# Five sums for four in layer 2, three joins for two in layer 1: moving 14 gathers of a graph network from GpSimd to TensorE

## The chip, the cores and the metric

The kernel runs on one NeuronCore of a Trainium2 chip. The metric is device time in microseconds (us) of one execution; lower is better. A core has five engines that run side by side, each with its own instruction stream: TensorE (PE in the profile; its weight loads are PEld), VectorE (DVE), ScalarE (ACT), GpSimd (POOL) and SyncE (SP). SP, ACT and GpSimd also issue DMA transfers, each in the order of its own stream. An instruction that waits for a semaphore holds up everything behind it in its stream.

## What is computed

Two layers of a relational graph convolution over 12,500 nodes with 128 features, 200,000 edges sorted by their target node `dst`, and 8 relations; then a residual sum and a layer norm.

```
def _rgcn_conv(x, src, dst, et, basis, comp, root, bias):
    W = jnp.einsum('rb,bio->rio', comp, basis)
    xw = jnp.einsum('ni,rio->nro', x, W)
    msgs = xw[src, et]
    seg = dst * N_REL + et
    summed = jax.ops.segment_sum(msgs, seg, num_segments=N_NODES * N_REL)
    cnt = jax.ops.segment_sum(jnp.ones((msgs.shape[0],), x.dtype), seg, num_segments=N_NODES * N_REL)
    mean = summed / jnp.maximum(cnt, 1.0)[:, None]
    agg = mean.reshape(N_NODES, N_REL, HIDDEN).sum(axis=1)
    return agg + x @ root + bias
...
h = x
for l in range(2):
    h_new = _rgcn_conv(h, src, dst, edge_type, basis[l], comp[l], root[l], bias[l])
    h = jax.nn.relu(h_new) + h
return _layernorm(x + h)
```

## The kernel before

**Tiles and quads.** The edges lie in 1563 tiles of 128, in their given order. Eight tiles make a quad, so there are 196 quads (0 to 195) in each layer, and each layer's main loop takes one quad a turn. For every edge a row of 128 floats is needed: in layer 1 the row of its source node in `x`, in layer 2 the row of source and relation in a table `y_d` that layer 1 writes to DRAM (each node's `h` times each relation's weight).

**The usual way to the rows: a gather.** `gather` (line 786) has GpSimd issue an indirect DMA for each tile, 128 rows picked by a column of indices, on line 814. A quad's rows go into one of seven buffers (`rows_r`, `AHEAD` + 2). `gathers` (line 837) writes the gathers of quad q + 5 into the program at turn q, so that of the seventh quad on waits until TensorE has used the buffer. For the last six quads (`NQ - LATE`, that is from quad 190 on) it is quad q + 2 that is written at turn q, and line 825 adds a wait for whatever quad TensorE was last told to use by then (the cell `("done", l)`).

**What TensorE does with them.** VectorE makes a weighted one-hot matrix of each tile's target nodes (`onehot`, line 1240: four quads' worth of buffers in layer 1, two in layer 2). In layer 1 `means` (line 1340) multiplies rows and one-hots, ACT copies the result, `product` (line 1372) multiplies with the relations' weights, ACT copies again and `place` (line 1403) adds to the node tile's sum; `table` (line 1558) makes the rows of `y_d`. In layer 2 `add_rows` (line 1726) multiplies rows and one-hots straight into the node tile's sum; `finish` adds the carry and the residual, and `norm` does the layer norm of eight node tiles at a time, whose result SP stores and whose buffer SP then loads with later rows of `x`.

**Three other ways to the rows**, each of which spares GpSimd its gathers:

- *Single-row lists* (`lists`, line 692; `lone_rows`, line 727). Every so many tiles a tile's 128 rows are fetched by 128 DMAs of one row each, issued by SP or by ACT (line 750) after a load of 32 addresses at a time (line 745). In layer 2 SP has tiles 62, 111, 160 and so on (every 49th, 31 tiles) and ACT has 63, 112 and so on. A chunk of 32 rows stands in the program up to 15 quads ahead of the quad that needs it; four tiles of a list have a place of their own (the halves of the buffers `sT`). `add_rows` waits for all the rows of its quad, these too.
- *Joins* in layer 1 (`JOINED`, `joining`, line 1475). For four tiles at once: the edges' sources are compared with the node numbers of each of the 98 node tiles (VectorE, line 1516), and each comparison is multiplied with that tile of `x` (TensorE, line 1531), which sums up the wanted rows. An entry holds the first tile served, and the first and last quad over which the 98 steps are spread. Two entries: eight tiles.
- *Sums* in layer 2 (`SUMMED`, `summed`, line 1586). The same for a whole quad, from `h` in SBUF: per node tile a transpose of `h` (TensorE, line 1610), its copy (VectorE, line 1618), a comparison of 1024 edges (line 1619), and two matmuls of 512 columns (line 1628); at the end the result is turned, multiplied with weighted one-hots and with the relations' weights. `52: (3, 45)` means that quad 52 is served by steps over quads 3 to 45. Four entries: 32 tiles.

**The order** on each engine is written out by the two loops at the end of `ordered_path`: what a turn calls first stands first in every engine's stream. `Plan.add` derives the waits from the cells that an operation reads and writes.

Of the kernel before, what the change touches and what calls it, by code (L numbers as in the profile page):

```python
# [428 lines left out]
def ordered_path(  # L429
# [26 lines left out]
    P = 128  # L456
# [11 lines left out]
    Q = 8  # L468
# [20 lines left out]
    SOON = 16  # L489
    DONE = NT - 4  # L490
    LONG = 9
    JOINED = [(1112, 84, 132), (1504, 135, 183)]
    SUMMED = {52: (3, 45), 98: (49, 91), 144: (95, 137), 190: (141, 183)}
    assert D == P and R * K == P and B == BF + 1 and 1 < TL and LAST < P and BF % 4 == 0 and Q == G and N % 2 == 0
    main = slice(HALO, HALO + P)

# [77 lines left out]
    def part_of(n, *cell):  # L574
        nonlocal free_at
        free_at += n
        assert free_at <= at
        used_c.append(cell)
        return arena[:, free_at - n:free_at], cell

    M = 4
    xb_b = [part_of(S * D, "xb", i) for i in range(2)]
    eqb_b = [part_of(M * P, "eqb", i) for i in range(4)]
    ends_b = part_of(M * P, "ends")
    joined_b = [part_of(M * P, "joined", i) for i in range(len(JOINED))]
    joined = {t + i: (joined_b[k][0][:, i * P:(i + 1) * P], [joined_b[k][1]])
              for k, (t, _, _) in enumerate(JOINED) for i in range(M)}
    room_c += used_c
    p_8 = keep([P, S + 2], F32, "p_8")
# [2 lines left out]
    first = keep([P, B], F32, "first")  # L592
# [86 lines left out]
    def floats(t, n):  # L679
        return t[:, n * P:(n + 1) * P]  # L680

    sT_f = [t.rearrange("p r g k -> p (r g k)") for t in sT_r.tiles]
# [6 lines left out]
    def hot_cells(c):  # L689
# [4 lines left out]
                                     (sel.rearrange("p g k -> p (g k)"), ["sel"], [])]),  # L694
         ("ACT", 13 * Q + 2, 46 * Q, 8 * Q, 16, 10, [(floats(yr_f, j), yr_cells, yr_cells) for j in range(5)]),
         ("ACT", 53 * Q + 2, 1552, 8 * Q, 16, 10, [(floats(mixer_f, j), ["mixer"], []) for j in range(2)])],
        [("SP", 62, 1552, 49, 32, 15, [(floats(sT_f[0], j), [("sT", 0, 0), ("sT", 0, 1)], []) for j in range(4)]),
         ("ACT", 63, 1552, 49, 32, 15, [(floats(sT_f[1], j), [("sT", 1, 0), ("sT", 1, 1)], []) for j in range(4)])]]
    single, at_row = [{}, {}], [0, 0]
    for l in range(L):  # L700
        for k, (_, t0, t1, by, _, _, hosts) in enumerate(lists[l]):
# [84 lines left out]
    def gather(l, q):  # L786
        if q >= NQ or l == 1 and q in SUMMED:
            return
# [433 lines left out]
    dms, sT, ys, pl, ym = {}, {}, {}, {}, {}  # L1222
    acc, carry, vs, xs, xT, wide = {}, {}, {}, {}, {}, {}

    def onehot(l, q, g=None):

        if q >= NQ and (g is None or g < 0) or l == 1 and q in SUMMED:
            return
# [246 lines left out]
    def joining(k):  # L1475

        tile0, first, end = JOINED[k]
        n = end - first + 1
        slots = [(g, i) for g in range(NX) for i in range(shape_of(g)[1])]
        assert len(slots) == NT  # L1480
        takes = {q: [] for q in range(first - 1, end + 3)}
        for j in range(NT):
            takes[first + j * n // NT].append(j)
        used = {g: [q for q, js in takes.items() if any(slots[j][0] == g for j in js)] for g in range(NX)}
        loads = {}
        for g in range(NX):
            loads.setdefault(max(first - 4 + g, JOINED[k - 1][2] + 2 if k else 0) if g < 2 else used[g - 2][-1] + 2, []).append(g)
        (e_t, e_c), (f_t, f_c), (j_t, j_c) = ends_b, eqb_b[0], joined_b[k]
        f3, j3 = (t.rearrange("p (t c) -> p t c", t=M) for t in (f_t, j_t))
        b, bc = ct_b  # L1490
        done = end + 1
        assert max(len(v) for v in takes.values()) <= 2
        assert tile0 // Q >= done + 3 and (k == 0 or first >= JOINED[k - 1][2] + 3)

        def load_b(g):
            p, m = shape_of(g)
            t, c = xb_b[g % 2]
            load(t[:p, :m * D], in_rows(x, g), [], [c] + (free_c if k == 0 and g < 2 else []), "ACT")

        def start_of(q):  # L1500
            if q == first - 4:
                assert checked and parts is None
                load(j_t.bitcast(I32), bass.AP(tensor=src.tensor, offset=src.offset + tile0 * P,
                                               ap=[[0, P], [1, M * P]]), [], [j_c] + free_c, "ACT")
            for g in loads.get(q, ()):
                load_b(g)

        def before(q):
            if q == first - 2 and k == 0:
                x_nodes()  # L1510
            if q == first:
                vec(lambda: nc.vector.tensor_copy(e_t, j_t.bitcast(I32)), [j_c], [e_c] + (free_c if k == 0 else []))
            for j in takes.get(q, ()):
                p = shape_of(slots[j][0])[0]
                o, oc = eqb_b[j % 4]
                vec(lambda j=j, p=p, o=o: nc.vector.tensor_tensor(  # L1516
                    o[:p], e_t[:p], x_node[:p, j:j + 1].to_broadcast([p, M * P]), op=ALU.is_equal),
                    [e_c, "x_node"], [oc])
            if q == done + 1:
                vec(lambda: nc.vector.tensor_copy(f3, b), [bc], [f_c])  # L1520
            if q == done + 2:
                vec(lambda: nc.vector.tensor_copy(j3, b), [bc], [j_c])
            plan.mark("DVE")

        def after(q):
            for j in takes.get(q - 1, ()):
                g, i = slots[j]
                p, m = shape_of(g)
                t, c = xb_b[g % 2]
                o, oc = eqb_b[j % 4]  # L1530
                pe(lambda j=j, p=p, i=i, t=t, o=o: nc.tensor.matmul(  # L1531
                    b.rearrange("p t c -> p (t c)"), t[:p, i * D:(i + 1) * D], o[:p], start=j == 0, stop=j == NT - 1),
                    [c, oc], [bc])
            if q == done + 1:
                pe(in_turn([lambda i=i: nc.tensor.transpose(b[:, i, :], f3[:, i, :], ident) for i in range(M)]),
                   [f_c, "ident"], [bc])
            plan.mark("PE")

        return start_of, before, after

    joins = [joining(k) for k in range(len(JOINED))]

    def join(o, part):
        for (_, first, end), f in zip(JOINED, joins):
            if first - 4 <= o <= end + 3:
                f[part](o)
# [135 lines left out]

    sums_of = [(s - 1, *summed(i, s, *SUMMED[s])) for i, s in enumerate(sorted(SUMMED))]

    def summing(q, part):
        for end, *f in sums_of:
            if SUMMED[end + 1][0] - LONG <= q <= end:
                f[part](q)
# [18 lines left out]
    def add_rows(q, k, opens, last, between_last=None):  # L1707
        if q in SUMMED:
            place_sums(q, k, opens, last)
# [159 lines left out]
    def run(gen, n):  # L1869
        for _ in range(n):  # L1870
            if next(gen, gen) is gen:
                return True
        return False
# [49 lines left out]
    later = checks()  # L1923
# [32 lines left out]
    for o in range(NG - 3):  # L1956
        if o + CLOSE == NQ - 2:
            gather(0, NQ - 1)
        gathers(0, o)
        means(o)  # L1960
        batch(o)
        join(o, 0)
        if o == 1:
            where()
            load_offsets()
        if o > 1:
            lone_rows(0, "SP", o)
        for i in range(2 if o < FIRST else 1):
            if parts is not None and run(parts, 1):
                parts = None  # L1970
        onehot(0, o + 2, o - 1)
        join(o, 1)
        if parts is None:
            run(later, 3 if o < 84 else 1)
        if o > 1:
            lone_rows(0, "ACT", o)
        if not opened:
            end()
        for step in opened:
            step()  # L1980
        opened.clear()
        if o > 0:
            product(o - 1)
            if o < SOLO:
                take_product(o - 1)
            else:
                late_y.append(o - 1)
        for step in behind:
            pe(*step)
            plan.mark("PE")  # L1990
        behind.clear()
        join(o, 2)
        if o > 1:
            k = place(o - 2)
            close(k)
            if k is not None and k % S == S // 2 and k // S + 1 < NX:
                n = k // S + 1
                turned_to.extend([turn_x(n, h) for h in range(-(-shape_of(n)[1] // 4))])
                turned_to.append((lambda n=n: load_x(n + 1), None))
        for i in range(2):  # L2000
            if turned_to:
                a, b = turned_to.pop(0)
            elif tables and o >= TABLE and (i == 0 or len(tables) > 6 or o > NG - 16):
                a, b = tables.pop(0)
            else:
                break
            while copies:
                copies.pop(0)(vcopy)
            a()
            if b is not None:  # L2010
                copies.append(b)
# [69 lines left out]
    for q in range(NQ):  # L2081
# [4 lines left out]
        k = sup(q)  # L2086
# [116 lines left out]
```

## Time and profile before

| what | value |
|---|---|
| three runs | 3728.68, 3730.01, 3738.03 us; median 3730.01 |
| the profiled execution's own time | 3738.43 us |
| its span, first to last instruction | 3736.6 us |
| busy share of PE, DVE, ACT, POOL | 80%, 63%, 9%, 75% |
| layer 1's gathers / layer 2's gathers | 1499 / 1469 |
| mean granted clock of TensorE | 0.937 |

How to read it: a group's row gives the line of the kernel, the engine, what is written from what, the count, then busy time and mean duration in ns, then the idle time of that engine just ahead of these instructions and what ended it. "issue" there means that the engine waited for nothing that the profile shows. A row of a line's or tile's view gives the count, the least, median and largest duration in ns, and when the first and the last began. A timeline's row gives the start, the length and what ran, neighbours of one kind merged; names with a q (SPq, ACTq) are an engine's sequencer issuing DMAs.

### The profile page before, as it was taken

How to read it: one execution, taken by the hardware profiler on the slowest of the kernel's cores; microseconds unless marked ns; L12 is line 12 of the kernel's file. 1: busy time of each engine (PE TensorE's matmuls, PEld its weight loads, DVE VectorE, ACT ScalarE, POOL GpSimd, SP SyncE). 2: the span in 40 equal slices, each digit the busy share in tenths (PEclk: the TensorE clock that was granted, in tenths of full speed). 3: DMA queues.
4: the chain of work that ended last, by engine and by line, in shares of the span. 5: the costliest groups of instructions: out<-in, count | busy, mean ns of one | idle time of the engine just before them, and what ended most of it. 6: DMA issues, size and time to landing. Idle time of an engine off the chain costs nothing.

```text
span 3736.6 us, 69352 instructions
## 1 busy us (share of the span) xinstructions
PE 2986.0 (80%) x13831; PEld 2137.2 (57%) x13831; DVE 2354.0 (63%) x5786; ACT 354.5 (9%) x795; POOL 2812.0 (75%) x2977
## 2 busy tenths in 40 slices
PE   5777757778877778877778888888888888798896
PEld 3666645565655556655555555555555555555554
DVE  5556435545554445445456778787777787787885
ACT  1121212111111111111100000000000000000000
POOL 7777777777777777777777777777777777777776
PEclk7999889989999999999989999999999999999998
DMA  4122123334333333332332222222222222222222
GB/s 126 55 62 61 56 89 106 117 115 123 112 101 100 91 104 106 95 106 92 99 97 56 55 56 67 67 62 67 56 73 62 62 67 62 67 66 56 68 66 61
DMA packets 159970, 299.91 MB, mean 80 GB/s; under 512 B 67108, under 2 KB 90358, under 8 KB 159534
## 3 DMA queue, kind: packets, MB, share of 16 engines
q0 software_dynamic: 95008, 194.77, 20.4%
q10 hardware_dynamic: 34755, 68.94, 5.7%
q1 hardware_dynamic: 29771, 31.73, 3.2%
q14 instruction: 325, 2.66, 0.2%
q8 instruction: 111, 1.82, 0.2%
HBM read 236.52 MB, written 58.65 MB: 79 GB/s over the span
## 4 chain that ended last, share of the span: by engine, by line
POOL 47%; issue 17%; PE 16%; DMA 9%; ACTq 4%; ACT 3%; DVE 2%; SPq 1%; POOLq 0%; DVEq 0%
POOL rows L814 47%; DMA rows<-y_d,idy 7%; PE y L1372 4%; ACTq L750 3%; PE s L1340 3%; PE s L1726 2%; PE pt L1558 1%; ACTq L745 1%; PE ct L1531 1%; ACT sT L663 1%; SPq L750 1%; ACT y_row L663 1%; DVE dm L1240 1%; PE ct L1010 1%; PE ct L1011 1%
## 5 line engine op out<-in xcount | busy, mean ns | idle before, releaser
L814 POOL DMA_INDIRECT rows<-in_x_dram,idx x1499 | 1420.0, 947 | 459.8 <-issue 451.1
L814 POOL DMA_INDIRECT rows<-y_d,idy x1469 | 1390.0, 946 | 449.8 <-issue 440.2
L1726 PE MATMUL s<-dm,rows 128*128 128x256 f32 x2932 | 777.2, 417 | 260.7 <-DMA rows<-y_d,idy 235.8
L1240 DVE TENSOR_SCALAR dm<-cols,near,w 128x256 f32<-128x256 f16 x1531 | 709.6, 537 | 386.1 <-PE s L1726 376.4
L1726 PEld LDWEIGHTS s<-dm,rows 128*128 128x128 f32 x2932 | 592.4, 210 | 376.4 <-DMA rows<-y_d,idy 233.7
L1240 DVE TENSOR_SCALAR dm<-cols,kr,w 128x128 f32<-128x128 f16 x1563 | 525.9, 403 | 137.4 <-PE s L1340 112.5
L1372 PE MATMUL y<-w_sb,sT 128*128 128x128 f32 x3136 | 443.8, 300 | 203.9 <-ACT ys L663 150.6
L1372 PEld LDWEIGHTS y<-w_sb,sT 128*128 128x128 f32 x3136 | 406.7, 209 | 240.3 <-ACT ys L663 177.6
L1340 PEld LDWEIGHTS s<-dm,rows 128*128 128x128 f32 x2998 | 382.2, 201 | 184.0 <-issue 159.1
L1340 PE MATMUL s<-dm,rows 128*128 128x128 f32 x2998 | 401.6, 287 | 100.5 <-DMA rows<-in_x_dram,idx 90.4
L1619 DVE TENSOR_TENSOR arena<-arena,cols 128x1024 f32<-128x1024 int32 x264 | 319.9, 1212 | 0.0
L1628 PE MATMUL pt<-arena,idx 128*128 128x512 f32 x528 | 269.6, 592 | 0.0
L1628 PE MATMUL y<-arena,idx 128*128 128x512 f32 x528 | 269.6, 592 | 0.0
L1558 PE MATMUL pt<-w_sb,arena 128*128 128x512 f32 (+1 forms) x386 | 206.3, 616 | 63.0 <-DVE y_row L666 43.9
L666 DVE COPY y_row<-pt 128x512 f32<-128x512 f32 x56 | 38.7, 692 | 309.9 <-PE pt L1558 309.9
L663 ACT ACTIVATE sT<-s 128x512 f32<-128x512 f32 x391 | 213.4, 605 | 87.0 <-PE s L1340 86.7
L1516 DVE TENSOR_TENSOR arena<-arena,cols 128x512 f32<-128x512 f32 (+1 forms) x196 | 125.7, 683 | 115.0 <-PE ct L1531 112.2
L1531 PE MATMUL ct<-arena 128*128 128x512 f32 x392 | 187.1, 600 | 0.0
L663 ACT ACTIVATE y_row<-pt 128x512 f32<-128x512 f32 (+1 forms) x139 | 83.0, 597 | 1044.1 <-PE s L1340 846.8
L1628 PEld LDWEIGHTS y<-arena,idx 128*128 128x128 f32 x528 | 100.3, 190 | 126.3 <-issue 126.3
L1619 DVE TENSOR_TENSOR y_row<-arena,cols 128x1024 f32<-128x1024 int32 x128 | 155.1, 1212 | 0.0
L1834 ACT ACTIVATE st<-st,eps 128x8 f32<-128x8 f32 x12 | 3.7, 310 | 1543.8 <-DMA sT<-y_d 1302.3
(253 smaller groups left out, 2300.0 us busy)
## 6 DMA issues: line engine op xcount, KB each, us to landing
sT<-y_d SPq DMA_DIRECT2D x3968, 0.5 KB
sT<-y_d ACTq DMA_DIRECT2D x3968, 0.5 KB
y_d<-y_row ACTq DMA_DIRECT2D x96, 512.0 KB
mixer<-in_x_dram ACTq DMA_DIRECT2D x2304, 0.5 KB
rows<-in_x_dram,idx POOLq DMA_INDIRECT x1499
rows<-y_d,idy POOLq DMA_INDIRECT x1469
jmp<-in_x_dram SPq DMA_DIRECT2D x1408, 0.5 KB
comp_sb<-in_x_dram SPq DMA_DIRECT2D x1408, 0.5 KB
```

Of the source, the lines that this page charges most:

```text
L663: act(lambda: nc.scalar.activation(out_t, in_t, AF.Copy), reads, writes)
L750: return [eng.dma_start(o[j * ch + i:j * ch + i + 1, :].bitcast(byte), table_b[bass.ds(v, 4 * D)].rearrange("(p d) -> p d", p=1)) for i, v ...
L814: ins.append(nc.gpsimd.indirect_dma_start(out=t[:, i - q * Q, :], out_offset=None, in_=table_t, in_offset=bass.IndirectOffsetOnAxis(ap=ids ...
L1240: emits.append(lambda i=i: nc.vector.tensor_scalar(t[:, i - q * Q, :wide], cols[:, :wide], ids[:, i:i + 1], w[:, i:i + 1], op0=ALU.is_equa ...
L1340: last = nc.tensor.matmul(s_b[i // 4][0][:, i % 4, :], lones[i][0] if i in lones else t[:, i, :], d[:, i, :], start=True, stop=True)
L1372: last = nc.tensor.matmul(y[:m], t[:, r, :nt, :].rearrange("p t k -> p (t k)"), w_sb[:, 0, r, :], start=(r == 0), stop=(r == R - 1))
L1516: vec(lambda j=j, p=p, o=o: nc.vector.tensor_tensor(o[:p], e_t[:p], x_node[:p, j:j + 1].to_broadcast([p, M * P]), op=ALU.is_equal), [e_c, ...
L1531: pe(lambda j=j, p=p, i=i, t=t, o=o: nc.tensor.matmul(b.rearrange("p t c -> p (t c)"), t[:p, i * D:(i + 1) * D], o[:p], start=j == 0, stop ...
L1558: pe(lambda: nc.tensor.matmul(hb[:n].rearrange("p r d -> p (r d)"), hT[:, j * P:j * P + n], w_sb[:, 1, k * H:(k + 1) * H, :].rearrange("p ...
L1619: vec(lambda j=j, e=e: nc.vector.tensor_tensor(e, edge, node_p[:, j:j + 1].to_broadcast([P, Q * P]), op=ALU.is_equal), [edge_c, "node"], h ...
L1628: pe(lambda j=j, m=m, o=o, e=e, h=h, b=b: nc.tensor.matmul(b.rearrange("p t c -> p (t c)"), o[:m], e[:m, 4 * h * P:4 * h * P + 4 * P], sta ...
L1726: ins = nc.tensor.matmul(a, lones[i][0] if i in lones else t[:, i, :], d[:, i, :], start=(opens and i == 0), stop=(last and i == n - 1 and ...
```

## The change

Layer 1 gets a third join of four tiles, layer 2 a fifth sum of eight, each spread over fewer quads than before (37 for 49, and 33 or 34 for 43). Layer 2's lists take every 47th tile, 32 on each queue. The two buffers of the joins are used in turn, the joins' matmuls stand ahead of the product in a turn, and the checks of the input run up to five steps a turn until quad 64.

```
-    JOINED = [(1112, 84, 132), (1504, 135, 183)]
-    SUMMED = {52: (3, 45), 98: (49, 91), 144: (95, 137), 190: (141, 183)}
+    JOINED = [(888, 70, 106), (1200, 109, 145), (1515, 148, 184)]
+    SUMMED = {44: (3, 36), 80: (40, 73), 117: (77, 110), 155: (114, 147), 191: (151, 183)}
...
-    joined_b = [part_of(M * P, "joined", i) for i in range(len(JOINED))]
-    joined = {t + i: (joined_b[k][0][:, i * P:(i + 1) * P], [joined_b[k][1]])
+    joined_b = [part_of(M * P, "joined", i) for i in range(2)]
+    joined = {t + i: (joined_b[k % 2][0][:, i * P:(i + 1) * P], [joined_b[k % 2][1]])
               for k, (t, _, _) in enumerate(JOINED) for i in range(M)}
...
-        [("SP", 62, 1552, 49, 32, 15, [(floats(sT_f[0], j), [("sT", 0, 0), ("sT", 0, 1)], []) for j in range(4)]),
-         ("ACT", 63, 1552, 49, 32, 15, [(floats(sT_f[1], j), [("sT", 1, 0), ("sT", 1, 1)], []) for j in range(4)])]]
+        [("SP", 62, 1552, 47, 32, 15, [(floats(sT_f[0], j), [("sT", 0, 0), ("sT", 0, 1)], []) for j in range(4)]),
+         ("ACT", 63, 1552, 47, 32, 15, [(floats(sT_f[1], j), [("sT", 1, 0), ("sT", 1, 1)], []) for j in range(4)])]]
...
-            if q == done + 1:
+            if q == done + 2:
                 pe(in_turn([lambda i=i: nc.tensor.transpose(b[:, i, :], f3[:, i, :], ident) for i in range(M)]),
                    [f_c, "ident"], [bc])
...
         batch(o)
         join(o, 0)
+        join(o, 2)
...
         if parts is None:
-            run(later, 3 if o < 84 else 1)
+            run(later, 5 if o < 64 else 1)
...
             plan.mark("PE")
         behind.clear()
-        join(o, 2)
```

More of the change, by code (lines that the diff above doesn't have):

```diff
@@ L1487, in joining @@
             loads.setdefault(max(first - 4 + g, JOINED[k - 1][2] + 2 if k else 0) if g < 2 else used[g - 2][-1] + 2, []).append(g)
-        (e_t, e_c), (f_t, f_c), (j_t, j_c) = ends_b, eqb_b[0], joined_b[k]
+        (e_t, e_c), (f_t, f_c), (j_t, j_c) = ends_b, eqb_b[0], joined_b[k % 2]
         f3, j3 = (t.rearrange("p (t c) -> p t c", t=M) for t in (f_t, j_t))
@@ L1491, in joining @@
         done = end + 1
-        assert max(len(v) for v in takes.values()) <= 2
+        assert max(len(v) for v in takes.values()) <= 3
+        assert k < 2 or first - 4 > JOINED[k - 2][0] // Q
         assert tile0 // Q >= done + 3 and (k == 0 or first >= JOINED[k - 1][2] + 3)
```

## The prediction

> **What bounds the kernel now.** I read the page first, for the engine with the largest share and for what ends its idle time.
>
> ```profile
> span 3736.6 us, 69352 instructions
> ...
> PE 2986.0 (80%) x13831; PEld 2137.2 (57%) x13831; DVE 2354.0 (63%) x5786; ACT 354.5 (9%) x795; POOL 2812.0 (75%) x2977
> ...
> L814 POOL DMA_INDIRECT rows<-in_x_dram,idx x1499 | 1420.0, 947 | 459.8 <-issue 451.1
> L814 POOL DMA_INDIRECT rows<-y_d,idy x1469 | 1390.0, 946 | 449.8 <-issue 440.2
> ```
>
> GpSimd (POOL) is busy for only 75%, yet its idle time is nearly all "issue": nothing that the profile shows held it. Busy and idle together, a gather of layer 1 costs (1420.0 + 459.8) / 1499 = 1.254 us and one of layer 2 (1390.0 + 449.8) / 1469 = 1.252 us. The view of line 814 shows that they follow each other from the first instruction to 13 us before the end, and the view of waits how little anyone holds them up:
>
> ```profile
> L814 POOL DMA_INDIRECT rows<-in_x_dram,idx x1499: 943/947/1248, 4.5 to 1881.1; - x188
> L814 POOL DMA_INDIRECT rows<-y_d,idy x1469: 943/947/1038, 1882.4 to 3722.9; - x184
> ...
> POOL rows L814 <- PE s L1726: 3.8, 9, 1.3
> ```
>
> So the kernel runs at GpSimd's pace in both layers, and a gather less is worth 1.253 us as long as nobody else is late. Who could be? TensorE (PE), VectorE (DVE), and the queues of SP and ACT that bring the single-row tiles. The windows of layer 2 give the first two:
>
> ```profile
> 1970.00:3690.00 1720.00, 1481.06 (x5242) 979.20 (x5241) 1316.37 (x2818) 4.69 (x12) 1299.57 (x1374) 0.95 0.27 63
> ```
>
> The columns are length, then PE, PEld, DVE, ACT and POOL busy, the granted clock, DMA share and GB/s: PE 86%, DVE 77%. The queues show in the view of line 750, whose times are those of layer 2's 31 tiles of 128 rows on each queue:
>
> ```profile
> L750 SPq DMA_DIRECT2D sT<-y_d x3968: 224/228/587, 1904.6 to 3639.6; - x199
> L750 ACTq DMA_DIRECT2D sT<-y_d x3968: 231/232/589, 1904.8 to 3596.3; - x199
> ```
>
> SP issues single rows for 1735 of layer 2's 1840 us. It is no idle helper, and this decides my forecast.
>
> **What goes.** Layer 1 loses four gathers (1499 to 1495). Layer 2 loses eight to the fifth sum, and two because each list has 32 tiles for 31 (1469 to 1459). 14 x 1.253 = 17.5 us, 5.0 of them before layer 2 begins: 3719 us of span if all else stays hidden.
>
> **What layer 1 gets.** A third join: 98 compares on DVE and 98 matmuls on PE. The rows are those of line 1531 and line 1516 up to 1882 us (two joins, 392 instructions for 196 matmuls), and of all work from 800 us on:
>
> ```profile
> 0.00:1882.00 1882.00, 187.12 (x392) 69.42 (x392) 0.93 0.32 96
> 0.00:1882.00 1882.00, 125.70 (x196) 0.93 0.32 96
> 800.00:1882.00 1082.00, 859.18 (x4798) 642.83 (x4798) 539.46 (x1472) 200.38 (x454) 818.12 (x865) 0.96 0.35 103
> ```
>
> One join is 94 us of PE and 63 us of DVE, beside 223 us of PE and 543 us of DVE idle there. Squeezed from 49 quads to 37 it takes up to three compares in a quad, and there are four buffers for them: DVE's second or third waits for PE to have used the quad before's. For that the joins' matmuls move ahead of the product, straight behind the means; there they fill the time in which ACT copies, so I cost the move at nothing. DVE behind such a wait holds the one-hots of two quads later, which gives it some 19 us. If the cover failed, PE would be late by at most one quad's matmuls, 3 x 0.94 us, with six quads of gathers in stock. The checks, run five a turn for three, are the same instructions earlier.
>
> **What layer 2 gets.** A fifth sum. The rows are lines 1628 and 1610 (PE) and 1619 and 1618 (DVE) over layer 2, four sums:
>
> ```profile
> 1882.00:3737.00 1855.00, 700.97 (x1568) 297.91 (x1568) 0.94 0.27 64
> 1882.00:3737.00 1855.00, 71.18 (x392) 53.14 (x392) 0.94 0.27 64
> 1882.00:3737.00 1855.00, 475.00 (x392) 0.94 0.27 64
> 1882.00:3737.00 1855.00, 111.59 (x392) 0.94 0.27 64
> ```
>
> PE gets (701 + 71) / 4 = 193 us, DVE (475 + 112) / 4 = 147 us. In the window above that makes PE about 1674 of 1707 us, 98%, and DVE 86%. I do not count this as PE the bound, because of what PE does when it need not wait:
>
> ```profile
> 2534.79 1.02 PE L1628 MATMUL y<-y_row,idx 128*128 128x512 f32 x2
> 2535.65 0.38 PE L1610 MATMUL ct<-ident,arena 128*128 128x128 f32 x2
> 2535.87 3.62 PE L1726 MATMUL s<-dm,rows 128*128 128x256 f32 x16
> ...
> 3684.60 5.51 PE L1726 MATMUL s<-dm,rows 128*128 128x256 f32 x14
> ```
>
> From start to start a half of a sum's step is 0.86 us and a transpose 0.11, a step 1.83; a quad's 16 matmuls take about 3.5, while 14 of them took 5.51 behind an idle stretch. A cycle of the new plan (37 quads, 36 of them gathered) asks 36 x 3.5 + 98 x 1.83 + some 15 for roots, norms and the sum's end = 320 us, where GpSimd takes 36 x 9.6 = 345 (9.6 being 1840 us over 192 gathered quads). PE is tight but ahead, and seven buffers let it lag six quads, 57 us. The Trainium skill ("TensorE: Matmul & The Clock Gate", "What's actually happening") says that an idle window of about 3.4 us halves PE's clock and a busy one restores it; the two rows agree (0.39 us a matmul against 0.23), and a fuller PE would be a faster one.
>
> **The single rows.** A tile more on each list. SP's timeline shows what a tile costs:
>
> ```profile
> 2272.24 0.38 SPq L660 DMA_DIRECT2D out_dram<-x_g  x1
> 2288.63 0.36 SPq L660 DMA_DIRECT2D x_g<-in_x_dram  x1
> 2291.22 48.71 SPq L750 DMA_DIRECT2D sT<-y_d  x128
> ...
> 3192.52 107.94 SPq L750 DMA_DIRECT2D sT<-y_d  x256
> ...
> 3589.74 50.13 SPq L750 DMA_DIRECT2D sT<-y_d  x128
> 3639.92 0.37 SPq L660 DMA_DIRECT2D x_g<-in_x_dram  x1
> ```
>
> After a pause 128 rows take 48.7 us, later 54 (107.94 / 2), so something behind the queue fills up; with the 2.6 us ahead of each tile, for its addresses, one is 51.3 to 55.3 us ((107.94 + 2.6) / 2), and I take 54. A store whose buffer is loaded next makes SP stand for 16.4 us; the written order has five such pairs ahead of SP's last tile before and four after. One pause less saves 16.4 us, but a pause also bought two or three fast tiles, some 7 us. So SP's last row goes from 3639.9 to 3639.9 - 5.0 + 54 - 9 = 3680.
>
> When is it needed? Its last tile is number 1519 (62 + 31 x 47), in quad 189. Every gather from quad 190 on waits for TensorE's newest quad at its place in the order (line 825): that of quad 192 for quad 189. The wait stands in the trace of before, on GpSimd's and on TensorE's timeline:
>
> ```profile
> 3690.39 0.95 POOL L814 DMA_INDIRECT rows<-y_d,idy  x1 [1.33 <-PE s L1726]
> ...
> 3683.16 1.22 PE L1726 MATMUL s<-dm,rows 128*128 128x256 f32 x2 [4.61 <-DMA rows<-y_d,idy]
> ```
>
> Quad 189 began on PE at 3683.2 and was done at 3690, and GpSimd went on at once with quad 192, standing 1.0 us beyond its 0.3: no slack. In the changed kernel this gather could start at 3690.4 - 17.5 = 3672.9. But tile 1519 has its last row issued at 3680 and landed 2 to 3 us later (estimate, from the 1.6 us between a quad's last gather and PE's start here), PE needs 6.8 us for the quad as here, and the gather starts at 3690, 17 us late. The same 27 gathers follow in both kernels. Of 17.5 us about 0.5 are left. The bounds of SP's last row: with 51.3 for the tile and the pause fully saved it is 3670, and the gather 7 us late; with 55.3 and nothing saved 3690, and 27 late. ACT's list, 43 us ahead of SP's at its end, stays ahead.
>
> Is the lateness only there? Two rows for the lists before:
>
> ```profile
> L1726 PE MATMUL s<-dm,sT x124: 379/379/454, 1971.3 to 3704.1; 128*128 128x256 f32 x124
> ...
> PE s L1726 <- DMA sT<-y_d: 3.8, 4, 1.7
> ```
>
> 124 matmuls on single-row tiles, and 3.8 us of waiting for them: the first tile stood at 1904.6 + 48.7 = 1953.3 for its use at 1971.3, the last some 60 us ahead. In the changed kernel 45 gathers lie between two tiles of a list, 56.4 us, less 10 us for each of the four summed quads in between; the queue needs 54 and its pauses. It gains some 2 us a tile and loses 10 at quads 44, 80, 117 and 155, so I expect waits for sT from the second or third of these on, up to 30 us of lateness, hidden by the seven buffers until quad 192.
>
> **The sum.** The profiled execution took 3738.43 us, span 3736.6; the median shown is 3730.01. Span: -17.5 + 17 = -0.5. On the median: 3729.5 us.
>
> **The rivals.**
> *The lists keep up.* Then all 17.5 us stay: 3712.5. For it: SP at 51.3 us a tile throughout would end near 3607 (1899.6 + 32 x 51.3 + 4 x 16.4). Against it: both queues slow down together, ACT also going from 50 to 54, as if one server stood behind both. The Trainium skill ("DMA: Bandwidth & Descriptors", "Issuing engines are not separate DMA queues") says that queues of different issuers share the same DMA engines and save only issue time; by that rule a second queue adds no service, and the trace agrees (54 us against 48.7). It decides from 3663 us for SP's last row. Chance 0.20.
> *TensorE lags beyond its buffers.* This ends slower. If PE keeps the cost of the window (98%) and half of its present 239 us idle cannot be used, it needs 1674 + 120 = 1794 of 1707 us, 87 too many; 57 fit into the buffers, GpSimd stands 30 us in the middle, and the end waits too: -17.5 + 30 + some 3 = +15, 3745. It decides where a quad's matmuls average over 4.2 us ((345 - 15 - 179) / 36). Against it are the 3.5 us of unhindered quads; for it, that late rows make PE idle and its clock fall. Chance 0.20.
> *GpSimd's own pace falls* with a fuller DVE: 0.5% of 1.253 us on 2954 gathers is 18 us, no gain, 3731 to 3740. Against it: 947 and 946 ns in layers with DVE at half and at three quarters. Chance 0.05. That the gathers do not go is excluded: the written program has 14 fewer.
>
> **The numbers.** The late list has 0.55; its own range is 3720 to 3740 by the bounds of SP's last row. 0.3% is 11 us, about what can be told from no change here. Faster by more needs SP's last row before 3670: the first rival and a little of the forecast, 0.25. Slower by more is the second rival and the forecast's tail, 0.22. The rest, 0.53, lies between. Leaving out half of each outer rival's spread, the range is 3712 to 3744.
>
> **What would show it.** Right: GpSimd's gathers gapless at 1.25 us, layer 2's first at 1877.4, then one gap of 15 to 20 us near 3673; SP's last single row at 3675 to 3688; PE waiting for sT. Wrong: no such gap and an end 17 us earlier (first rival), or waits of GpSimd for PE strewn over 2400 to 3600 (second).

## The result, and the profile after

| | before | after |
|---|---|---|
| median of 11 runs each | 3730.23 us | 3738.39 us |
| lowest to highest | 3728.68 to 3738.03 | 3733.03 to 3742.22 |
| the profiled execution | 3738.43 us | 3736.4 us |

The ratio is 1.0019, with a 95% interval of 1.0011 to 1.0026: some 8 us slower, where no change was forecast. The two profiled executions stand the other way round (the changed one is 2 us shorter), and this is the first thing to clear up. The page of the changed kernel, the view of line 814, the view of line 750 and the view of waits, beside those in the prediction:

```profile
span 3734.6 us, 71627 instructions
...
PE 3147.7 (84%) x14547; PEld 2198.4 (59%) x14547; DVE 2542.5 (68%) x6091; ACT 354.4 (9%) x795; POOL 2792.2 (75%) x2963
```

```profile
L814 POOL DMA_INDIRECT rows<-in_x_dram,idx x1495: 940/944/1286, 4.7 to 1872.5; - x187
L814 POOL DMA_INDIRECT rows<-y_d,idy x1459: 940/944/1053, 1873.7 to 3721.6; - x183
```

```profile
L750 SPq DMA_DIRECT2D sT<-y_d x4096: 224/228/601, 1896.5 to 3683.2; - x196
...
L750 ACTq DMA_DIRECT2D sT<-y_d x4096: 231/232/555, 1896.6 to 3648.3; - x196
```

```profile
PE ct L1611 <- DVE arena L1620: 90.5, 6, 34.8
...
DVE arena L1620 <- DMA arena<-in_src_dram: 55.2, 2, 33.6
DVE st L1839 <- ACT st L1835: 54.6, 5, 25.1
...
POOL rows L814 <- PE s L1727: 28.4, 15, 16.5
...
PE s L1727 <- DMA sT<-y_d: 1.1, 1, 1.1
```

A row of waits gives the total, the number and the longest one, in us. The 14 gathers are gone (1495 and 1459), SP's last single row went from 3639.6 to 3683.2, and GpSimd waits 28.4 us for TensorE where it was 3.8. (Of the 14, twelve went to TensorE, by the join and the sum; the other two went to the lists of SP and ACT.) Where GpSimd stands is in its timeline:

```profile
3047.09 0.94 POOL L814 DMA_INDIRECT rows<-y_d,idy  x1 [1.90 <-PE s L1727]
...
3056.25 0.94 POOL L814 DMA_INDIRECT rows<-y_d,idy  x1 [1.97 <-PE s L1727]
...
3675.91 0.94 POOL L814 DMA_INDIRECT rows<-y_d,idy  x1 [16.45 <-PE s L1727]
...
3689.10 0.94 POOL L814 DMA_INDIRECT rows<-y_d,idy  x1 [4.75 <-PE s L1727]
```

The last stop is the one that was forecast: the first gather of quad 192 (the last 27 gathers start here) waits for quad 189. The longest one stands seven gathers earlier, at the first of quad 190, the first gather that line 825 holds back. The two short ones near 3050 lie in the middle of the layer, where a gather waits only until TensorE has used its buffer, the seventh back. So TensorE was late well before quad 192, and not for want of single rows (1.1 us in all). The view of waits names two waits of VectorE that the kernel before hardly had: for a load of `src`, which the comparisons of the sums need (line 1620; called an edge load below), and for ACT's square root in the layer norm (line 1835). First SP, VectorE and TensorE at the longer wait for an edge load, then ACT and VectorE at the longest wait for a root:

```profile
2980.01 26.91 SPq L750 DMA_DIRECT2D sT<-y_d  x69
3006.97 0.37 SPq L660 DMA_DIRECT2D arena<-in_src_dram  x1
```

```profile
3022.42 1.22 DVE L1620 TENSOR_TENSOR arena<-arena,cols 128x1024 f32<-128x1024 int32 x1 [33.63 <-DMA arena<-in_src_dram]
```

```profile
3026.36 0.90 PE L1611 MATMUL ct<-ident,arena 128*128 128x128 f32 x3 [34.75 <-DVE arena L1620]
```

```profile
2334.97 162.02 ACTq L750 DMA_DIRECT2D sT<-y_d  x384
2497.04 0.31 ACT L1835 ACTIVATE st<-st,eps 128x8 f32<-128x8 f32 x1 [164.15 <-DMA sT<-y_d]
```

```profile
2497.38 0.20 DVE L1839 RECIPROCAL st<-st 128x8 f32<-128x8 f32 x1 [25.14 <-ACT st L1835]
```

SP issues the edge load only when the rows written ahead of it are out, ACT takes the root between two stretches of rows, VectorE stands for either, and TensorE behind VectorE. The edge load is late twice over: of VectorE's 33.6 us some 18 passed before it was issued at 3007.0, and another 15 until VectorE went on. So a late list costs time though TensorE hardly ever waits for a row.

### The profile page after: what moved, and what is told of

Its sections match the earlier page's. It is cut to its first block, busy times and chain, and to the rows that moved or that the text cites. A ratio compares the mean times of both kernels' runs of the same rounds, so it can differ in the third digit from the quotient of the medians.

```text
span 3734.6 us, 71627 instructions
## 1 busy us (share of the span) xinstructions
PE 3147.7 (84%) x14547; PEld 2198.4 (59%) x14547; DVE 2542.5 (68%) x6091; ACT 354.4 (9%) x795; POOL 2792.2 (75%) x2963
## 4 chain that ended last, share of the span: by engine, by line
PE 33%; POOL 28%; issue 13%; ACTq 12%; SPq 6%; DMA 4%; DVE 3%; ACT 2%; POOLq 0%; DVEq 0%
POOL rows L814 28%; ACTq L750 10%; PE s L1727 9%; PE y L1629 7%; PE pt L1629 7%; SPq L750 5%; ACTq L745 2%; PE s L1340 2%; PE y L1372 2%; SPq L745 1%; DMA rows<-y_d,idy 1%; DMA rows<-in_x_dram,idx 1%; DMA arena<-in_src_dram 1%; PE pt L1559 1%; DVE dm L1240 1%
## 5 line engine op out<-in xcount | busy, mean ns | idle before, releaser
L1727 PE MATMUL s<-dm,rows 128*128 128x256 f32 x2912 | 710.5, 392 | 64.8 <-DMA rows<-y_d,idy 51.0
L1727 PEld LDWEIGHTS s<-dm,rows 128*128 128x128 f32 x2912 | 553.7, 198 | 147.5 <-DMA rows<-y_d,idy 39.2
L1340 PEld LDWEIGHTS s<-dm,rows 128*128 128x128 f32 x2990 | 383.8, 203 | 237.8 <-issue 220.6
L1517 DVE TENSOR_TENSOR arena<-arena,cols 128x512 f32<-128x512 f32 (+1 forms) x294 | 193.9, 680 | 379.6 <-PE ct L1532 379.5
L1620 DVE TENSOR_TENSOR arena<-arena,cols 128x1024 f32<-128x1024 int32 x330 | 398.7, 1208 | 55.2 <-DMA arena<-in_src_dram 55.2
L1629 PE MATMUL pt<-arena,idx 128*128 128x512 f32 x660 | 337.0, 592 | 0.0
L1629 PE MATMUL y<-arena,idx 128*128 128x512 f32 x660 | 337.0, 592 | 0.0
L1532 PE MATMUL ct<-arena 128*128 128x512 f32 (+1 forms) x588 | 282.1, 613 | 0.0
L1619 DVE COPY idx<-ct 128x128 f32<-128x128 f32 x490 | 138.7, 283 | 100.3 <-PE ct L1611 97.9
L1620 DVE TENSOR_TENSOR y_row<-arena,cols 128x1024 f32<-128x1024 int32 x160 | 193.2, 1208 | 0.0
L1629 PEld LDWEIGHTS pt<-arena,idx 128*128 128x128 f32 x660 | 125.3, 190 | 99.3 <-issue 92.3
```

Of the source, the lines that this page charges most:

```text
L1340: last = nc.tensor.matmul(s_b[i // 4][0][:, i % 4, :], lones[i][0] if i in lones else t[:, i, :], d[:, i, :], start=True, stop=True)
L1517: vec(lambda j=j, p=p, o=o: nc.vector.tensor_tensor(o[:p], e_t[:p], x_node[:p, j:j + 1].to_broadcast([p, M * P]), op=ALU.is_equal), [e_c, ...
L1532: pe(lambda j=j, p=p, i=i, t=t, o=o: nc.tensor.matmul(b.rearrange("p t c -> p (t c)"), t[:p, i * D:(i + 1) * D], o[:p], start=j == 0, stop ...
L1620: vec(lambda j=j, e=e: nc.vector.tensor_tensor(e, edge, node_p[:, j:j + 1].to_broadcast([P, Q * P]), op=ALU.is_equal), [edge_c, "node"], h ...
L1629: pe(lambda j=j, m=m, o=o, e=e, h=h, b=b: nc.tensor.matmul(b.rearrange("p t c -> p (t c)"), o[:m], e[:m, 4 * h * P:4 * h * P + 4 * P], sta ...
L1727: ins = nc.tensor.matmul(a, lones[i][0] if i in lones else t[:, i, :], d[:, i, :], start=(opens and i == 0), stop=(last and i == n - 1 and ...
```

## The experiments

Each stands against runs of the kernel before on the same chip.

**The kernel before once more.** Nothing is edited.

> The kernel before, once more, for a second profile of it. Its first profiled execution took 3738.4 us where the median of its runs is 3730.2. If the 8 us are GpSimd's own pace, this one shows gathers about 1.249 us apart (1.252 in the first profile) and a span near 3728; if they are a stall somewhere, the pace is 1.252 again and the difference stands in another row.

3730.33 us. Its view of line 814, of line 750, and GpSimd's timeline at quad 192:

```profile
L814 POOL DMA_INDIRECT rows<-y_d,idy x1469: 940/944/1050, 1880.0 to 3714.8; - x184
```

```profile
L750 SPq DMA_DIRECT2D sT<-y_d x3968: 224/228/634, 1900.9 to 3639.4; - x199
```

```profile
3682.35 0.94 POOL L814 DMA_INDIRECT rows<-y_d,idy  x1 [0.30 <-PE s L1698]
```

The gathers are 3 ns shorter than in the execution on which the prediction rests (least and median 940/944 for 943/947), on 2968 gathers 8.9 us, and the last one starts at 3714.8 for 3722.9. SP's list ends where it ended then (3639.4 and 3639.6). So the first profiled execution had GpSimd's slower pace; that the runs around the median all have the faster one is inferred from this one trace of them.

**The parts of the change.** Three kernels, each with one part: the third join with the new order; the fifth sum with lists at 49; the lists at 47 with four sums and two joins.

```
joins:  SUMMED and the lists as before
sums:   JOINED and the code as before;  ("SP", 62, 1552, 49 -> ("SP", 72, 1552, 49,  ACT 73
lists:  all as before but  ("SP", 62, 1552, 49 -> ("SP", 61, 1552, 47,  ACT 62
```

> The change's layer 1 alone: three joins for two, their matmuls moved ahead, the checks at five a turn; sums and lists of layer 2 as before. Four gathers fewer. If layer 1 hides its third join: 4 x 1.25 = 5 us faster, 3725 us. If the denser joins cost something: 3730 or more, with gaps in layer 1's gathers.

> The fifth sum alone: lists stay at every 49th tile, 31 on each queue, but begin ten tiles later (72 and 73) since tile 356 would fall into the newly summed quad 44; joins as before. Eight gathers fewer. Theory 1, the last single row of SP sets the end: it is out of the way at this spacing, so 8 x 1.25 = 10 us faster, 3720. Theory 2, VectorE waits for loads and square roots that stand behind single rows in the queues, and TensorE cannot catch up: such waits remain but are shorter, 3722 to 3730. Theory 3, the fifth sum alone is more than TensorE can carry: gaps of GpSimd from quad 30 on, 3735 or more.

> The denser lists alone: every 47th tile, 32 on each queue (from tile 61 and 62), four sums and two joins as before. Two gathers fewer. Theory 1: SP's last row comes near 3680, quad 189 is used about 12 us late, and the end is 5 to 10 us later than before, 3735 to 3740. Theories 2 and 3: TensorE has 14% idle and catches up, 2.5 us faster, 3727.5.

Against 3730.43: the join 3725.92 (ratio 0.9987, 0.9978 to 0.9996), four gathers less, 4.5 us; the sum 3719.67 (0.9972, 0.9961 to 0.9983), 10.8 us, both as expected; the lists 3741.63 (1.0033, 1.0021 to 1.0046), 11.2 us slower although two gathers are gone, which is a little beyond the range of the first theory. The waits and GpSimd's timeline of the kernel with the lists alone:

```profile
PE s L1726 <- DMA sT<-y_d: 75.0, 10, 13.7
...
DVE st L1838 <- ACT st L1834: 66.2, 9, 19.8
...
DVE arena L1619 <- DMA arena<-in_src_dram: 58.3, 3, 37.0
```

```profile
3688.17 0.94 POOL L814 DMA_INDIRECT rows<-y_d,idy  x1 [18.62 <-PE s L1726]
```

With four sums the lists at 47 are already late: the fifth sum is not what they need. The three parts add up to -4.1 us, the whole change measured +8.2: they do not add up, and with the lists at 47 the gains of the other two parts are lost.

**The lists put back.** The changed kernel with its five sums and three joins, but lists at 49.

```
-        [("SP", 62, 1552, 47, ...    ("ACT", 63, 1552, 47, ...
+        [("SP", 72, 1552, 49, ...    ("ACT", 73, 1552, 49, ...
```

> The changed kernel with lists at every 49th tile, 31 on each queue, from 72 and 73, run again. If the parts add up as measured alone (4.5 and 10.8 us): 3715. If a TensorE with both is too full: 3718 to 3725.

3716.65 against 3732.11 (0.9958, 0.9945 to 0.9972): 15.5 us faster than before, the join's and the sum's gains together (15.3), and 12 gathers of 1.249 us (15.0).

```profile
POOL rows L814 <- PE s L1727: 4.4, 14, 0.4
...
DVE st L1839 <- ACT st L1835: 0.4, 1, 0.4
```

All the new waits are gone (GpSimd's 4.4 us are 14 of the usual 0.3, and TensorE waits 0.7 us for single rows), with TensorE as full of sums as in the changed kernel. This is the fastest of all kernels here, and it shows where the loss comes from: the denser lists. It is their spacing and not the tile more, for a kernel with 31 tiles at 47 (the second of the next three) stays slow.

**Which of the waits?** First the edge loads 18 quads ahead for nine; then the lists without their last tile (the one that quad 189 needs); then both.

```
early2:      -LONG = 9   +LONG = 18
drop2:       ("SP", 62, 1552, 47 -> ("SP", 62, 1500, 47,  ACT 63 the same
dropearly2:  both
```

> The changed kernel with the sums' edge lists loaded 18 quads ahead for 9, run again where the kernel before takes its usual 3730 us. As for the first run: theory 1, SP's last single row sets the end and stays near 3683 us, time within 2 us of the changed kernel, 3737 to 3739; theory 2, the waits behind the single rows set it, 3730 or less.

> The changed kernel without the last tile of each list of layer 2 (1519 and 1520 are gathered), run again. Theory 1: about 17 us less than the changed kernel less 2.5 for two more gathers, 3724. Theory 2: TensorE comes as late to quad 187 as before and the stop for quad 190 stays, 3734 to 3738.

> Edge lists 18 quads ahead and the last tile of each list gathered, run again. Both theories: 3715 to 3719. Above 3724 a third cause is left, the waits for square roots behind ACT's single rows or TensorE's own load.

Against 3732.11 they took 3738.24 (1.0016, 1.0007 to 1.0025), 3736.93 (1.0011, 1.0002 to 1.002) and 3737.16 (1.0009, 1.0 to 1.0018). None brings the 15 us back, also not the third, for which both theories had 3715 to 3719. The waits of the first, GpSimd's two stops in the second, and the waits of the third with GpSimd's timeline:

```profile
DVE st L1839 <- ACT st L1835: 70.6, 7, 25.2
...
PE s L1727 <- DMA sT<-y_d: 43.0, 10, 10.6
...
POOL rows L814 <- PE s L1727: 32.2, 16, 20.3
```

```profile
3673.36 0.94 POOL L814 DMA_INDIRECT rows<-y_d,idy  x1 [15.06 <-PE s L1727]
...
3685.26 0.94 POOL L814 DMA_INDIRECT rows<-y_d,idy  x1 [2.22 <-PE s L1727]
```

```profile
DVE st L1839 <- ACT st L1835: 71.7, 8, 22.7
...
PE s L1727 <- DMA sT<-y_d: 39.7, 8, 12.2
```

```profile
3677.15 0.94 POOL L814 DMA_INDIRECT rows<-y_d,idy  x1 [18.52 <-PE s L1727]
```

With the edge loads early, no wait for them is left, and TensorE waits for the rows themselves (1.1 us before, 43.0 now) and VectorE longer for the root. Without the tile that the forecast made the culprit, the stop at quad 190 is about as long as ever (15.06 us in the second kernel, 18.52 in the third, for 16.45), and of the stop at quad 192 2.22 us are left for 4.75. So neither of the two is the cause by itself: the list as a whole is late, and whoever stands nearest behind it waits.

**What limits a list?** SP's list alone (the kernel before without ACT's layer-2 list, whose 31 tiles go back to GpSimd), and the changed kernel with the loads of later rows of `x` written a fixed number of quads on, so that SP doesn't stand 16 us behind a store. On the chip of these and the next two runs the kernel before took 3738.24 us, and the traces of all four have GpSimd's slower pace (median 947 ns).

```
sponly:  the entry ("ACT", 63, 1552, 49, ...) left out
moved:   -todo.extend([lambda: None] * 2 + [lambda n=n: load_x(n + 2)])
         +due.setdefault(min(q + 22, NQ - 5), []).append(n + 2)     # called at that turn
```

> The kernel before without ACT's list in layer 2 (its 31 tiles are gathered instead, 39 us more). Only SP's pace per tile is asked. If SP and ACT share a server behind them: with ACT silent SP never slows down, every tile stays at 48.5 to 49.5 us. If SP's slower tiles (52 to 54 us) are its own, they appear again some 150 us after each pause.

> The changed kernel with each load of x that SP issues in layer 2 put 22 quads after its norm began for some 16, so that SP need not stand for the landing of a store just ahead of it: the four pauses of 16.4 us go, the rows stay the same. Shared server: SP's last row comes some 30 us earlier, near 3650, but ACT's comes later by as much, near 3680 for 3649; the lists are still late as a whole, 3725 to 3738. Separate servers: SP earlier and ACT as before, lists in time but for a few us, 3713 to 3720.

With SP alone: 3775.65 against 3738.24, 37.4 us for 31 gathers more (38.7). SP's timeline of seven tiles there, then of the same stretch in the changed kernel:

```profile
1905.06 353.62 SPq L749 DMA_DIRECT2D sT<-y_d  x896
...
3430.84 100.27 SPq L749 DMA_DIRECT2D sT<-y_d  x256
```

```profile
1896.49 370.57 SPq L750 DMA_DIRECT2D sT<-y_d  x896
```

Without ACT's list a tile takes 50.5 us with its address loads (353.62 / 7) for 52.9, and late in the layer still 50.1 where with both lists 53 to 54 are usual. SP's pauses shrink too. These are SP's waits for a store in the kernel before, and with SP's list alone:

```profile
SPq L660 <- DMA out_dram<-x_g: 81.8, 6, 16.1
```

```profile
SPq L660 <- DMA out_dram<-x_g: 14.7, 6, 2.7
```

So most of the 16 us goes when ACT's rows go: the store seems to stand in one backlog with the rows of both queues, and so may the edge load that took 15 us. No run takes this apart further.

The kernel with the loads moved took 3752.73 (1.0038, 1.0024 to 1.0052), which neither theory had expected: 14 us slower than before, and by the ratio worse than the change itself. Its view of line 750, waits, and GpSimd's timeline:

```profile
L750 SPq DMA_DIRECT2D sT<-y_d x4096: 227/228/574, 1899.4 to 3657.9; - x196
...
L750 ACTq DMA_DIRECT2D sT<-y_d x4096: 231/234/632, 1899.5 to 3679.6; - x196
```

```profile
DVE st L1839 <- ACT st L1835: 115.9, 9, 29.3
...
POOL rows L814 <- PE s L1727: 37.5, 12, 26.6
...
DVE arena L1620 <- DMA arena<-in_src_dram: 13.2, 1, 13.2
```

```profile
3693.28 0.94 POOL L814 DMA_INDIRECT rows<-y_d,idy  x1 [26.65 <-PE s L1727]
```

SP's pauses are gone and its list ends 25 us earlier, but ACT's ends 31 us later (3679.6 for 3648.3), as expected of a shared server: what SP gained, ACT lost, and SP's pauses had been ACT's free time. TensorE never waits for single rows here; what stands ahead of GpSimd's stop of 26.65 us is 115.9 us of VectorE's waiting for roots, beside one edge load of 13.2.

These rows give the pace of the pair with no pause on either side: (3657.9 - 1899.4) / 32 = 55.0 us for a tile on SP's queue and (3679.6 - 1899.5) / 32 = 55.6 on ACT's, address loads included, 55.3 on the mean. With SP's pauses the changed kernel has 55.8 and 54.7, and the kernel before, by its rows in the prediction, 56.0 and 54.6: again 55.3 on the mean. So the pair gets through a tile on each queue every 55.3 us, pauses or not, and the pauses only decide which of the two queues is behind.

What is asked for follows from the gathers between two tiles of a list. At 47, from tile 62 to tile 1519, these are 1457 tiles less 62 of single rows and 32 of sums, 1363 x 1.249 / 31 = 54.9 us: less than the pair needs. At 48 it is 55.8 (1386 gathers in 31 steps), at 49 57.0 (1370 in 30). By this sum the lists at 47 cannot keep up, and those at 48 just can if neither queue has to carry pauses.

**One tile more apart.** The changed kernel at 48, as it is and with the loads moved.

```
after48:   ("SP", 62, 1552, 47 -> ("SP", 62, 1552, 48,  ACT 63 the same
after48m:  the same, with the edit of the kernel with the loads moved
```

> The changed kernel with lists at every 48th tile from the same first tiles: again 32 tiles on each queue and 14 gathers fewer than before, but the last tiles stand in quad 193 for 189, and six of SP's pauses come ahead of its last row. Lateness by the queue's pace: in the middle the lists hold (56.2 us of gathers and summed quads per tile against 55.4), but SP's last row comes near 3700 for a use at 3685: 3725 to 3735. If spacing alone decides: 3713.

> Every 48th tile, and the loads of x put later so that SP's pauses go. Lateness by the queue's pace: SP's last row near 3650, ACT's near 3680, both in time for quad 193: all 17.5 us of the 14 gathers, 3713 to 3716. If TensorE with five sums is the limit after all: 3720 or more.

Against 3738.24 they took 3746.26 (1.0021, 1.0012 to 1.003) and 3725.88 (0.997, 0.9958 to 0.9982), both slower than the pace had let me expect (3725 to 3735, and 3713 to 3716). First TensorE's timeline and the waits of the former, then the waits of the latter:

```profile
3384.21 0.90 PE L1611 MATMUL ct<-ident,arena 128*128 128x128 f32 x3 [41.35 <-DVE arena L1620]
```

```profile
DVE arena L1620 <- DMA arena<-in_src_dram: 45.6, 1, 45.6
...
POOL rows L814 <- PE s L1727: 32.6, 16, 17.0
```

```profile
DVE st L1839 <- ACT st L1835: 34.3, 7, 6.6
...
POOL rows L814 <- PE s L1727: 8.8, 14, 4.1
```

At 48 with SP's pauses, one edge load that stood behind 154 us of SP's rows goes with it: TensorE stands for 41 us, and GpSimd pays 32.6, of which the 17.0 come some 300 us later, at quad 190. With the pauses taken out, the pair keeps up by the sum above, the waits are short, and 12.4 us of the 14 gathers' 17.5 are kept. The expectation had put 3720 and more down to TensorE as the limit; but with the same five sums and lists at 49 TensorE held up nobody. So the same edit pays 20 us at 48, where at 47 it brought nothing (1.0038 for 1.0019, on two chips): the two sides of the 55.3 us.

**What did not decide.** Six runs came from two chips on which the kernel before itself took 5695.74 and 5621.2 us. On the one: the first attempts at early edge loads, at the dropped tile, at both and at lists of 49 in the changed kernel. On the other: two kernels with ACT's root written three turns earlier, so that eight turns lie between root and reciprocal for five, one of them with early edge loads too.

> The changed kernel with the sums' edge lists loaded 18 quads ahead of their first step for 9, so that this load no longer stands among the single rows that come too late. Its two waits of VectorE for that load (33.6 and 21.6 us) should go. Theory 1, SP's last single row sets the end: that row stays near 3683 us, GpSimd stands in one place for quad 192 instead of for 190 and 192, time within 2 us of the changed kernel, 3737 to 3739. Theory 2, the waits behind the single rows make TensorE late and that sets the end: 8 us or more faster, 3730 or less.

> The changed kernel without the last tile of each list of layer 2: 31 tiles on each queue, still every 47th; tiles 1519 and 1520 are gathered. Two gathers more, 2.5 us. Theory 1: the stop for quad 192 goes whole, about 17 us less, 3724. Theory 2: TensorE comes to quad 187 as late as before (24 us), the 16.5 us stop for quad 190 stays and with it most of the time, 3734 to 3738.

> Both: the edge lists loaded 18 quads ahead, and the last tile of each list gathered. Both theories hold that neither of the two lateness is left at the end: 12 gathers fewer than before are 15 us, 3715 to 3719. If it stays above 3724, the waits for square roots or TensorE's own load are a third cause.

> The changed kernel with lists at every 49th tile, 31 on each queue, from tile 72 and 73: the joins and the sums without the denser lists. If the two parts add up as measured alone (4.5 and 10.8 us): 3715. If a TensorE with both is too full: 3718 to 3725.

> The changed kernel with the norm's root (ACT) written three turns earlier and its reciprocal (DVE) where it was, so that eight turns (some 77 us) lie between them for five (48). Both theories: DVE's waits for the root (54.6 us in the changed kernel) fall under 10. If those waits delay TensorE beyond repair, 10 to 20 us of GpSimd's stop near 3675 go with them, though the two waits for edge loads (55 us) stay: 3730 to 3735 where the changed kernel took 3738. If the rows of the lists are late by themselves, TensorE waits for sT instead and it is 3736 to 3739.

> The same with the edge loads issued 18 quads ahead for nine: neither wait behind the rows is left. If those waits were the price, GpSimd's stop near 3675 falls under 5 us, only the stop of quad 192's gather for SP's last tile stays (10 to 17 us), and it takes 3722 to 3730. If the queues' pace itself is the limit, TensorE waits for sT by 40 us or more in all, the stop near 3675 stays at 10 to 20, and it takes 3734 to 3739 as with early edge loads alone.

5729.61 (1.007, 1.0046 to 1.0095), 5693.38 (0.9998, 0.9973 to 1.0022), 5691.41 (1.0001, 0.9978 to 1.0024), 5651.98 (0.9927, 0.9902 to 0.9952), 5615.79 (0.9998, 0.998 to 1.0015) and 5621.16 us (1.0, 0.9984 to 1.0017). Here a tile of 128 rows took 68 to 98 us in SP's timelines; two of them in that of the kernel with the earlier root alone:

```profile
3908.50 87.60 SPq L750 DMA_DIRECT2D sT<-y_d  x128
...
4169.64 80.13 SPq L750 DMA_DIRECT2D sT<-y_d  x128
```

Both layers are half as long again (layer 1's last gather starts at 2763.3 us), and what was to be told apart drowns in that: four show no change, early edge loads alone were slower, and only lists at 49 were faster there too. How much of the price in the changed kernel would stay with neither wait for an edge load nor for a root behind the rows is therefore open.

## Why the prediction was wrong

**Right: GpSimd's pace as the currency.** Fewer gathers were worth 1.1 to 1.35 us each wherever nobody was late (4.5 us for 4, 10.8 for 8, 15.5 for 12). The third join is hidden, as said, and layer 2 began at 1873.7.

**Right: TensorE is not the bound, and more easily than I worked out.** The window of the changed kernel that answers to the one of before:

```profile
1970.00:3690.00 1720.00, 1580.91 (x5744) 1021.19 (x5743) 1447.30 (x3029) 4.68 (x12) 1281.90 (x1358) 0.96 0.29 63
```

TensorE is at 92% where I summed up 98, mostly because its matmuls got shorter (those of line 1726 from 417 to 392 ns on the mean) while it was idle less, and with lists at 49 it stays ahead. The second rival (TensorE beyond its buffers by its own work) fell with that run. But "seven buffers let it lag six quads, 57 us" was too kind: right behind the wait of 35 us at 3026 GpSimd stood twice for a buffer (1.90 and 1.97 us), and an engine at 92% had not made up its waits by 3676 (from 3639.5 to 3669.9 its timeline shows no wait: it was still working off what had piled up).

**Right in size by luck, wrong in cause: the stop near the end.** I put SP's last row at 3680 (3683.2), ACT's ahead of it (3648.3), and one stop of 17 us near 3673 (16.45 us until 3675.9). That the sizes agree is chance: I explained the stop by the last tile reaching quad 189, and this tile has a share only in the later stop of 4.75 us. Quad 189 stood there for its rows for 1.06 us:

```profile
3684.91 0.67 PE L1727 MATMUL s<-dm,rows 128*128 128x256 f32 x2 [1.06 <-DMA sT<-y_d]
```

The step "hidden by the seven buffers until quad 192" failed: what a late list holds up is not only TensorE's wait for `sT`, which stayed at 1.1 us, but the edge loads in SP's stream and the roots in ACT's. They made TensorE late from the middle of the layer on, and line 825 has GpSimd wait for TensorE from quad 190's gathers on, not only at quad 192's. I had counted what SP's rows cost SP, and never listed what else is queued behind them.

**Right: one server behind both queues.** The 54 us that I took for a tile were near the 55.3 that each queue needs when both run. That "a second queue adds no service" was a wrong reading of 54 against 48.7, though: the pair brings two tiles in 55.3 us where SP alone brings one in 50.1, 1.8 times as many rows. The Trainium skill says ("DMA: Bandwidth & Descriptors", "Issuing engines are not separate DMA queues") that queues of several issuers run on the same engines; the run with SP's list alone (50.1 us late in the layer) and that with the loads moved (SP 25 us earlier, ACT 31 us later) agree. By the same page ("Why a DMA increments its semaphore by 16 and not by 1") SP's and ACT's DMAs that use only some of the engines use the lowest-numbered ones. Whether the server is one such engine stays open: no view here shows which engine a row took.

**Wrong: from the profiled execution to the median.** I worked the sum against 3738.43 us, found -0.5, and carried this over to the median: 3729.5. As an absolute time the sum held: 3737.9, and the changed kernel's median is 3738.39. What failed is the last step, "On the median: 3729.5 us". The profiled execution was 8.4 us over the median, and the run of the kernel before once more showed why: GpSimd's pace. A kernel that GpSimd bounds has these 8 us back in the other runs. The changed one is late by its lists, and a list keeps the queues' pace whatever GpSimd's is (SP's ended at 3639.6 and 3639.4 in the two executions of the kernel before; two such traces of the changed kernel are not at hand). Against the faster execution the sum reads: quad 192's gather could start at 3682.35 - 14 x 1.249 = 3664.9, it started at 3689.1, 24.2 us late for the 17 forecast, and -17.5 + 24.2 = +6.7. GpSimd's four stops, each less the usual 0.30, come to 23.9 of these 24.2. The profiled executions differ by 6.1 (3736.4 - 3730.33), the medians by 8.2. The row that should have warned me was in the table: two of the three runs were at 3729 and 3730, and the profile was of the third kind.

## What to carry to other kernels

Before a queue gets more work, set its service time beside the demand, for all queues that share the server together: here a service of 55.3 us stood against demands of 54.9, 55.8 and 57.0 at spacings of 47, 48 and 49, and taking a pause from one queue only gave it to the other. Then list everything that stands in the same streams behind the added transfers, small loads and single activations too, for their waits come before those for the transfers themselves. And where the profiled execution is not at the median, ask which engine's pace made the difference, and whether the changed kernel is still bound by that engine.

## What the runs showed of the hardware

GpSimd's time for the same indirect DMA differs from execution to execution by some 3 ns of 944: its median is 944 or 945 ns in some traces and 947 in others, the same in both layers of one execution; on 2968 gathers that is 0.24% of the time. Two queues of single rows together get through 1.8 times the rows of one, at 55.3 us for 128 rows on each, and SP stood 13.6 us on the mean for a store behind them (81.8 / 6), 2.5 with its own rows alone (14.7 / 6). And rows issued one by one differ far more between chips than the gathers do: 49 to 54 us for 128 of them on two chips, 80 to 88 in the timeline shown above, from a third, where the gathers' median is 947 ns as elsewhere.
